# A three-layer graph network on one core: the head's loads put on one queue, and the list of layer 0 set out anew

## The chip, the core and the metric

The kernel runs on one core of a Trainium2 chip. The core has five engines with an instruction stream each: TensorE (PE, with its weight loads PEld), VectorE (DVE), ScalarE (ACT), GpSimd (POOL) and SyncE (SP). SP, ACT and POOL can issue transfers; the transfers run on the core's 16 DMA engines. The metric is the device time of one execution in microseconds (us), as the median over runs of the same kernel. The profile is of one execution of its own.

## The reference

The input is x (2500 nodes of 256 features, float32) and 80,000 edges, src to dst, sorted by dst. Cut to what matters:

```
h = max(layernorm(x), 0); xs = [h]
for W, b in layers 0, 1, 2:                  # W is 512 x 256
    m = concat(h[dst], h[src] - h[dst]) @ W + b
    h = relu(segment_sum(m, dst) / max(count(dst), 1))
    xs.append(h)
out = x + concat(xs) @ Wf + bf
```

No edge list is walked for the messages. With W split into an upper half Wt (for h[dst]) and a lower half Wb (for h[src]), a layer is relu((A z)/count + h (Wt - Wb)), where z = h Wb and A is the 2500 x 2500 matrix of how often each edge occurs. So the kernel builds A once, out of the sorted edges, and uses it in all three layers.

## The kernel before, in words

The work is done by `by_windows` (from L353). `general` (L18) is a fallback that runs only if a count does not add up; nothing of it runs here. Nodes lie in 20 tiles of 128; the code speaks of 10 pairs of tiles, q = 0 to 9. The columns of A (the dst side) are cut into 417 windows of 6 nodes, and these into 5 groups (GWS, four of 84 windows and one of 81); the last group is called "alone" later on.

**The head** has two strands that run side by side up to some 35 us.

The strand of the nodes: x is loaded into `acc` in five chunks of tiles (0-1, 2-5, 6-11, 12-15, 16-19; L443). For each pair: `st` takes mean and variance on DVE (BATCH_NORM_STATS2 and BATCH_NORM_AGGREGATE, tile `st` and `mv`); `sq`, `sc`, `of` turn the variances of a group of pairs into scales on ACT and DVE (groups: pair 0; pair 1; pairs 2-3; 4-7; 8-9); `N`, `Nd`, `Nm`, `Np` normalize the two tiles on POOL, DVE or ACT; `T` transposes them on PE, `R` takes them to `hT` with the relu on ACT; `Z` and `F` are the products with the layer's Wb and with Wf's first part (own_w), each 8 matmuls; `H`, `L` split Z's result into a high part zh (ACT) and a low part zl (DVE), `G` copies F's result into `acc` (ACT).

The strand of the edges: dst is loaded whole as 128 rows of 625 (`dst_i`). `first` and `next` compare row ends, `pi`, `pk`, `sg`, `se` search for the first edge of each block of windows (there are four blocks); `start_i` is the result, `ge` fetches a block's edges with two indirect transfers issued by POOL (`ed`, `es`), `aw`, `ka`, `kb`, `kr`, `km`, `kw`, `kc`, `kt`, `k1`, `k2` turn them into keys. From the keys, `B` makes one-hot tiles on DVE (`one_m`, `one_n`), `C` multiplies them on PE, and `E` copies the counts into A on ACT (`a`). `dstr` and `io` are casts on ACT (dst_i into `dst_r`; index rows).

**What sets the order.** There is no scheduler at work on the compute engines: every operation goes through the wrapper `InOrder` (its line, L267, stands in nearly all rows of the profile), and two strings, `order` and `later` (L920 and L1165), list the steps. Each engine runs the parts of the steps that are its own, in the order of the list, and waits on semaphores for what the other engines do. A short string `PICKS` (L372) says which bank of PSUM each product takes, and `WARM` says ahead of which steps PE runs matmuls on a tile `idle` that only keep it busy. POOL has both the normalizing steps and the indirect transfers in one stream.

**The rest of layer 0** is the string `later`: `g` opens a group of columns, `u` multiplies one tile of nodes into it (4 matmuls of zh and zl against `a`), `o` adds a node's own term, `r` ends the group (relu into `hT`); `c`, `e`, `b` go on with counts, copies and one-hots for the next groups; `f` finishes a group's `a` and writes it to `a_dram` through POOL's queue; `d`, `y`, `p`, `s`, `w`, `l` prepare node degrees, own terms and weights. `k` issues four loads of the next weights from SP into tiles that the one-hots no longer need (`one_m`, `one_n`); `v` makes three forms of the fourth of them, which `q` (products of the last two pairs) needs; `g` of the last group also has SP load the bias `bf_sb`, into memory that group 3's `a` held; `x` has POOL add five tiles of x onto `acc` by a transfer; `h` writes the result of `q` to `acc`.

**Layers 1 and 2** read A back from `a_dram` (tile `staged`), make `block` tiles of it and multiply; the change does not touch their text. Layer 1 begins at about 187 us.

The head's loads, in the order of the program (L432 to L475): ACT's queue issues dst_i and x's tiles 6-11; SP's queue issues x's tiles 0-1 and 2-5, Wb of layer 0, tiles 12-15, Wf's first part, tiles 16-19 (two transfers), Wt of layer 0.

Of the kernel before, what the change touches and what calls it, by code (L numbers as in the profile page):

```python
# [298 lines left out]
def by_windows(ctx: ExitStack, tc: tile.TileContext, x, src, dst, Ws, bs, Wf, bf, out, missing):  # L299
    nc = tc.nc  # L300
    PE, DVE, ACT, POOL, SP = nc.tensor, nc.vector, nc.scalar, nc.gpsimd, nc.sync
    PEo, DVEo, POOLo, ACTo, SPo = (InOrder(tc, e) for e in (PE, DVE, POOL, ACT, SP))
# [57 lines left out]
    class Banks:  # L360
# [9 lines left out]
    left = ctx.enter_context(ExitStack())  # L370
    right = ctx.enter_context(ExitStack())
    PICKS = {  # L372
        "right": "012313013012310102103210321032103210321032103210321032103210321032103210321032103210321032103210321032103210321031",
        "odd": "01010101011010",
        "even": "010101010101101010101010101001100110101010",
    }
    ps_right = Banks(right.enter_context(tc.tile_pool(name="ps_right", bufs=1, space=PSUM, side="right")), 4, PICKS["right"])
    ps_two = [Banks(left.enter_context(tc.tile_pool(name=f"ps_{k}", bufs=1, space=PSUM)), 2, PICKS[k]) for k in ("odd", "even")]
# [52 lines left out]

    dst_rows = dst.rearrange("(p c) -> p c", p=P)  # L432
    dst_i = pp.tile([P, R], I32, name="dst_i")
    ACTo.dma_start(dst_i, dst_rows)
# [9 lines left out]
    load_x(SPo, *chunks[0])  # L444
    load_x(SPo, *chunks[1])
    load_x(ACTo, *chunks[2])
    ws = [None] * L
    wfs = [None] * (L + 1)
    raws = [None] * (L + 1)
# [21 lines left out]
    load_wb(0, SPo)  # L471
    load_x(SPo, *chunks[3])
    load_wf(0, SPo)
    load_x(SPo, *chunks[4])
    load_wt(0, SPo)  # L475

# [57 lines left out]
    first = pp.tile([P, 1], F32, name="first")  # L534
# [358 lines left out]
    def by_count(g):  # L893
# [24 lines left out]
        "B": compare, "C": counts, "E": lambda b: take_counts(b, a),  # L918
    }
    order = """  # L920
        dstr lim first st0 sq0 next pi0 pk00 sc0 pk01 pi1 sg00 of0 Nm0 T0 st1 se00 sg01 pk10 st2 se02 R0 sq1 sc1
        of1 sg10 se01 se03 pk21 sg21 Z0 Np1 pk31 sg31 st4 T1 st7 pk30 sg30 st6 st5 F0 st8 R1 sq3 sc3 pk20 sg20
        se04 pk11 Z1 sg11 Nd7 pb0 T7 se10 ge0 G0 aw0 of3 se11 st3 R7 F1 se12 N6 T6 sa0 se13 ge1 H0 ge3 st9 ka0
        io kr0 kb0 sq4 sc4 km0 kw0 se14 R6 G1 Nm5 F7 kc0 kt0 k10 k20 pb1 of4 Np8 Nm9 L0 G7 H1 T5 R5 sa1 B0 B1 B2
        aw1 F6 G6 B3 kr1 ka1 Z6 kb1 H6 C0 kw1 E0 C1 T9 E1 ka3 sq2 ge2 R9 km1 T8 R8 sc2 B5 B4 L6 Z5 C2 H5 C3 E2
        E3 Z9 L5 C5 N2 C4 kc1 of2 aw2 V9 aw3 L1 E5 km3 H9 E4 B7 B6 T2 Z7 kr2 R2 kt1 k21 ka2 kb2 k11 C6 E6 N4 Z2
        km2 kr3 C7 kb3 kw2 C8 Nm3 T4 E7 kw3 E8 kc2 kc3 T3 B9 kt2 R3 k12 k22 kt3 k23 k13 L9 B8 B11 Z8 B12 C10 H2
        C9 L2 B13 Z3 C11 C12 E10 F3 H7 R4 E9 E12 E11 C13 G3 C14 E14 E13 B10 F5 L7 B15 C16 H8 B17 B19 B16 C15 E15
        G5 L8 E16 Z4 H4 L4 C18 C17 E17 F4 H3 C20 C19 E18 F2 E20 E19
        """  # L930

    second = ctx.enter_context(ExitStack())
# [56 lines left out]
    E12 = 4096.0  # L989
    C1 = 1.0 + 1.0 / E12  # L990
# [160 lines left out]
    def take_next(it=iter(range(len([b for b in windows if b[0] == 0]), len(windows)))):  # L1151
# [11 lines left out]
        "h": each((late_final, (q,)) for q in LATE),  # L1163
    }
    later = """  # L1165
        g d d d B18 u G4 u B23 d d u u G2 u B21 d u B24 ws c e e e e B14 B22 B20 b L3 u d d d b b d u u u c d y
        e e o e o b u b c o o e e u e e w e f b c u u b b d e e e e u c b b d d u u u d w e e e e u c d e d d u
        b b c r g u e u e b w e u u c w b b e y e e e d u u p x u u u c d u u u o e e b b f c e e e b b d o p e
        e e e u u u c d d d u u u o u o b e e b e e c e d b b d u d d r g c e u u u e e y u b b u u u c d d u u
        p u u u b e e e c b y d d b b e o f u c b e e o u e u e e e e u u p d c o d o e e e e b c e e e f d b d  # L1170
        b u u u c b b p r b g u u u u c x u o u u e b b o u u u e c e e e e e e p e o x b b e e e u u u c u u b
        b e c e e o e u b s y b c e e e e u e f k v v v v u u l u r g u s u u u u u u p u q o q o u s p u u o u
        q u u q u u u o u u u n n n n h s h x r l
        """
    acts.update(steps)
    for name in (order + later).split():
# [272 lines left out]
    for l in range(1, L):  # L1449
# [66 lines left out]
    for i, q in enumerate(order):  # L1516
# [30 lines left out]
def gnn_kernel(tc: tile.TileContext, x, src, dst, Ws, bs, Wf, bf, out):  # L1547
    nc = tc.nc
    with tc.tile_pool(name="flag", bufs=1) as flag:
        missing = flag.tile([1, 1], I32, name="missing")  # L1550
        tc.mark_branch_hint_location("again", "LikelyTaken",
                                     engines=[getattr(mybir.EngineType, e) for e in ("PE", "DVE", "Activation")])
        near_end = by_windows(tc, x, src, dst, Ws, bs, Wf, bf, out, missing)
        loads, (again,) = nc.values_load_multi_w_load_instructions(missing, min_val=0, max_val=1)

        for d in loads:
            if d.ins.engine in [getattr(mybir.EngineType, e) for e in ("PE", "DVE", "Activation")]:
                tc.add_manual_dep(d.ins, near_end.ins.name,
                                  mybir.DependencyInfo(mybir.DependencyClass.Sync, mybir.DependencyReason.DATA),
                                  reason="behind the outputs")  # L1560
        with tc.If(again > 0, label="again"):
            general(tc, x, src, dst, Ws, bs, Wf, bf, out)
# [28 lines left out]
```

## Time and profile before

| what | value |
|---|---|
| runs | 458.28, 458.49, 459.91 us; median 458.49 |
| profiled execution | 458.63 us, of which the span from first to last instruction is 456.5 us |
| PE busy | 449.2 us (98% of the span) |
| PEld, DVE, ACT, POOL busy | 358.2, 372.8, 318.9, 43.6 us |
| granted PE clock | 1.000 over the span |
| moved by DMA | 52.47 MB, 115 GB/s over the span; 277 GB/s in the first of 40 slices (11.4 us) |

The page names engine, operation, `out<-in` by the program's tiles, the count of instructions, and idle time with what ended it. Matmuls are pipelined, so their durations overlap, and the start of one against the start of the next tells more than the duration. "SPq", "ACTq" and "POOLq" are the issuing of transfers by these engines. A wait is put down to the one thing that came last by the profile.

### The profile page before, as it was taken

What the parts mean: (1) busy time and instruction counts of PE and PEld (TensorE: products, weight loads), DVE (VectorE), ACT (ScalarE), POOL (GpSimd) and SP (SyncE); (2) the same over time, 40 slices, a digit from 0 to 9 for tenths busy, and PEclk for the clock granted to TensorE, in tenths of its full rate; (3) what the DMA queues carried; (4) which work ended last, traced back from release to release, by engine and by line L of the source; (5) the groups of instructions that cost most, each with busy time, mean ns of one, the idle gap of its engine ahead of it and who ended that gap; (6) DMA issues with size and microseconds to landing.
All of it is one profiled execution on the core that took longest, in us unless ns stands there. A gap on an engine that the chain in (4) does not pass through costs nothing.

```text
span 456.5 us, 7452 instructions
## 1 busy us (share of the span) xinstructions
PE 449.2 (98%) x2737; PEld 358.2 (78%) x2737; DVE 372.8 (82%) x724; ACT 318.9 (70%) x586; POOL 43.6 (10%) x64
## 2 busy tenths in 40 slices
PE   8999999999999999999999999999999999999996
PEld 4888877888888888878878868867888787688685
DVE  6999999998899555379979859876999687569796
ACT  5898878777764535397779849756877897497540
POOL 4790101101022010100000000000000000000000
PEclk9999999999999999999999999999999999999999
DMA  8310266833719985611495522011124855220015
GB/s 277 115 36 1 51 122 111 157 79 70 151 36 192 154 199 103 145 47 45 123 378 204 182 90 93 0 45 47 46 54 142 326 184 180 90 92 1 1 53 176
DMA packets 22056, 52.47 MB, mean 115 GB/s; under 512 B 1931, under 2 KB 12382, under 8 KB 22014
## 3 DMA queue, kind: packets, MB, share of 16 engines
q1 hardware_dynamic: 14654, 33.83, 22.2%
q0 software_dynamic: 5856, 16.48, 19.0%
q10 hardware_dynamic: 1504, 1.63, 1.1%
q8 instruction: 22, 0.36, 0.3%
q14 instruction: 20, 0.16, 0.1%
HBM read 36.47 MB, written 15.62 MB: 114 GB/s over the span
## 4 chain that ended last, share of the span: by engine, by line
PE 89%; DMA 3%; POOL 3%; DVE 3%; ACT 1%; issue 1%; ACTq 0%; POOLq 0%
PE bank L267 89%; DMA acc<-in_x_dram 2%; POOL acc L267 1%; DMA staged<-a_dram 1%; DVE st L267 1%; POOL es L267 1%; POOL ed L267 1%; DVE acc L267 0%; DVE staged L267 0%; DVE mv L267 0%; ACT block L267 0%; DVE tmp L267 0%; ACT tmp L267 0%; DVE zl L267 0%; ACT zh L267 0%
## 5 line engine op out<-in xcount | busy, mean ns | idle before, releaser
L267 ACT CAST block<-staged 128x1008 fp32r<-128x1008 bf16 x120 | 117.9, 1031 | 18.9 <-DVE staged L267 6.5
L267 PE MATMUL bank<-block,zh 128*128 128x504 f32 (+1 forms) x200 | 83.7, 418 | 0.0
L267 PE MATMUL bank<-a,zh 128*128 128x504 f32 (+1 forms) x200 | 80.3, 401 | 0.0
L267 PE MATMUL bank<-a,zl 128*128 128x504 f32 (+1 forms) x200 | 77.9, 389 | 0.0
L267 PE MATMUL bank<-block,zl 128*128 128x504 f32 (+1 forms) x200 | 77.2, 386 | 0.0
L267 ACT CAST a<-bank 128x480 fp32r<-128x480 f32 (+1 forms) x105 | 53.0, 568 | 26.6 <-PE bank L267 26.6
L267 PE MATMUL bank<-block,sh 128*128 128x504 f32 x160 | 69.1, 432 | 0.0
L267 DVE TENSOR_TENSOR one_m<-iota_m,key_m 128x2048 bf16<-128x2048 bf16 (+2 forms) x55 | 63.9, 1162 | 5.9 <-PE bank L267 5.9
L267 PE MATMUL bank<-block,staged 128*128 128x512 f32 (+1 forms) x288 | 62.8, 369 | 0.2 <-DVE staged L267 0.2
L267 PE MATMUL bank<-block,sl 128*128 128x504 f32 x160 | 62.5, 391 | 0.0
L267 PEld LDWEIGHTS bank<-block,staged 128*128 128x128 f32 x288 | 49.3, 189 | 10.6 <-DVE staged L267 0.8
L267 DVE TENSOR_TENSOR block<-staged 128x1008 fp32r<-128x1008 bf16 x40 | 46.9, 1204 | 5.3 <-PE bank L267 3.9
L267 PEld LDWEIGHTS bank<-block,zh 128*128 128x128 f32 x200 | 37.6, 188 | 10.8 <-issue 2.1
L267 PEld LDWEIGHTS bank<-block,zl 128*128 128x128 f32 x200 | 37.6, 188 | 10.5 <-issue 3.5
L267 PEld LDWEIGHTS bank<-a,zl 128*128 128x128 f32 x200 | 37.7, 188 | 7.4 <-issue 0.5
L267 PEld LDWEIGHTS bank<-a,zh 128*128 128x128 f32 x200 | 37.6, 188 | 7.5 <-issue 0.5
L267 DVE TENSOR_TENSOR one_n<-iota_n,key_n 128x640 bf16<-128x640 bf16 (+2 forms) x110 | 42.7, 429 | 0.0
L267 PEld LDWEIGHTS bank<-block,sh 128*128 128x128 f32 x160 | 30.1, 188 | 10.5 <-issue 3.5
L267 PEld LDWEIGHTS bank<-block,sl 128*128 128x128 f32 x160 | 30.1, 188 | 9.3 <-issue 3.7
L267 DVE TENSOR_TENSOR staged<-staged 128x1008 bf16<-128x1008 bf16 x40 | 27.1, 679 | 12.0 <-ACT block L267 11.6
L267 PEld LDWEIGHTS <-one_m 128*128 128x128 bf16 x834 | 29.1, 98 | 7.3 <-issue 4.3
L267 PE MATMUL bank<-own_w,hT 128*128 128x256 f32 x144 | 34.7, 385 | 0.0
(192 smaller groups left out, 645.2 us busy)
## 6 DMA issues: line engine op xcount, KB each, us to landing
staged<-a_dram SPq DMA_DIRECT2D x52, 504.0 KB
a_dram<-a POOLq DMA_DIRECT2D x20, 630.0 KB, 9.0
acc<-in_x_dram POOLq DMA_DIRECT2D x3, 640.0 KB, 17.2
out_dram<-acc SPq DMA_DIRECT2D x5, 256.0 KB
acc<-in_x_dram SPq DMA_DIRECT2D x2, 512.0 KB
acc<-in_x_dram ACTq DMA_DIRECT2D x1, 768.0 KB
out_dram<-acc SPq DMA_DIRECT2D x5, 128.0 KB
wt<-in_L_gnn_W_dram SPq DMA_DIRECT2D x2, 256.0 KB
```

Of the source, the lines that this page charges most:

```text
L267: return self.tc.keep_in_program_order(call(*args, **kwargs))
```

## The change

The two transfers on ACT's queue go to SP's queue, and the order there becomes: tiles 0-1, dst_i, tiles 2-5, Wb, tiles 6-11, Wf's first part, tiles 12-15, tiles 16-19, Wt. The two strings that list layer 0's steps, and the string of PSUM banks, are replaced by others. The same steps are in them; `order` as a whole now ends with the copies of the counts, and pair 2's product F2 has gone over into `later`.

```
     "right": the picks from the 11th on
     "odd":   "01010101011010"           ->  "01010100100101"
     "even":  the picks from the 17th on
 dst_i = pp.tile([P, R], I32, name="dst_i")
-ACTo.dma_start(dst_i, dst_rows)
...
 load_x(SPo, *chunks[0])
+SPo.dma_start(dst_i, dst_rows)
 load_x(SPo, *chunks[1])
-load_x(ACTo, *chunks[2])
...
 load_wb(0, SPo)
-load_x(SPo, *chunks[3])
+load_x(SPo, *chunks[2])
 load_wf(0, SPo)
+load_x(SPo, *chunks[3])
 load_x(SPo, *chunks[4])
 load_wt(0, SPo)
...
 order = """
-dstr lim first st0 sq0 next pi0 pk00 sc0 pk01 pi1 sg00 of0 Nm0 T0 st1 se00 sg01 pk10 st2 se02 R0 sq1 sc1
+lim first dstr io st0 next pi0 pk00 sq0 sc0 of0 pk01 Nm0 sg00 pi1 st1 sg01 T0 R0 st5 sq1 sc1 se00 se02
...
 later = """
-g d d d B18 u G4 u B23 d d u u G2 u B21 d u B24 ws c e e e e B14 B22 B20 b L3 u d d d b b d u u u c d y
+g ws G4 d d L4 d d F2 G2 d d d u u u B24 u B14 B22 u c e B20 u u e e b e d d d u u u b c e u u u b b c d
...
-b e c e e o e u b s y b c e e e e u e f k v v v v u u l u r g u s u u u u u u p u q o q o u s p u u o u
-q u u q u u u o u u u n n n n h s h x r l
+c e e e u u e o u c e s u p u u r g u f o o b k u u u u v u u u u u v v l q n q s p s n n n u u u u u
+q h u u u o q h x o s u u l r x
```

What it makes of three engines' streams:

SP, the loads of the head, as they stood before (own_w_131 is Wb, own_w_134 Wf's first part; dst_i and the 6 tiles were on ACT):

```order
L267 DMA acc<-in_x_dram 128x2x256
L267 DMA acc<-in_x_dram 128x4x256
L267 DMA own_w_131<-in_L_gnn_W_dram 128x2x256
L267 DMA acc<-in_x_dram 128x4x256
L267 DMA own_w_134<-in_L_gnn_Wf_dram 128x2x256
L267 DMA acc<-in_x_dram 128x3x256
L267 DMA acc<-in_x_dram 68x256
L267 DMA wt<-in_L_gnn_W_dram 128x2x256
```

and as they stand in the change:

```order
L267 DMA acc<-in_x_dram 128x2x256
L267 DMA dst_i<-in_dst_dram 128x625
L267 DMA acc<-in_x_dram 128x4x256
L267 DMA own_w_130<-in_L_gnn_W_dram 128x2x256
L267 DMA acc<-in_x_dram 128x6x256
L267 DMA own_w_133<-in_L_gnn_Wf_dram 128x2x256
L267 DMA acc<-in_x_dram 128x4x256
L267 DMA acc<-in_x_dram 128x3x256
```

The chunk of six tiles now stands fifth of one stream, behind dst_i, tiles 2-5 and Wb.

DVE, from the end of pair 1's statistics to the first `start_i` (block 0's) and a little on, before (st and mv are the statistics, end_f the search):

```order
L267 TENSOR_SCALAR end_f_199<-row_204 128x1
L267 BN_STATS st_275<-acc_85 128x6
L267 BN_STATS st_277<-acc_85 128x6
L267 BN_AGGR mv_205<-st_275 128x2
L267 BN_AGGR mv_205<-st_277 128x2
L267 SCALAR_TENSOR_TENSOR end_f_199<-base_197,end_f_199 128x1
L267 RECIPROCAL rs_206<-rs_206 128x2
L267 SCALAR_TENSOR_TENSOR off_207<-mv_205,rs_206 128x2
L267 SCALAR_TENSOR_TENSOR end_f_199<-base_197,end_f_199 128x1
L267 TENSOR_SCALAR start_i_202<-end_f_199,least_203 128x1
L267 BN_STATS st_308<-acc_85 128x6
```

and in the change:

```order
L267 BN_AGGR mv_205<-st_276 128x2
L267 BN_AGGR mv_205<-st_278 128x2
L267 RECIPROCAL rs_206<-rs_206 128x2
L267 TENSOR_SCALAR end_f_199<-row_204 128x1
L267 SCALAR_TENSOR_TENSOR end_f_199<-base_197,end_f_199 128x1
L267 SCALAR_TENSOR_TENSOR off_207<-mv_205,rs_206 128x2
L267 SCALAR_TENSOR_TENSOR end_f_199<-base_197,end_f_199 128x1
L267 BN_STATS st_299<-acc_85 128x6
L267 BN_STATS st_301<-acc_85 128x6
L267 BN_AGGR mv_205<-st_299 128x2
L267 BN_AGGR mv_205<-st_301 128x2
L267 TENSOR_SCALAR start_i_202<-end_f_199,least_203 128x1
```

Before, the pair that follows pair 1 here is pair 2 (tiles 4-5, of the chunk 2-5), and the first row that needs the six tiles is st_308 (pair 4). In the change st_276 and st_278 are pair 5 (tiles 10-11, of the six) and st_299, st_301 pair 4, so that the end of the search and `start_i` now stand behind the statistics of two pairs of that chunk. Pair 2 comes after pairs 6 and 7.

SP, the loads that layer 0's `later` issues, before:

```order
L506 DMA dst_e<-outer 1x128
L267 DMA one_m<-in_L_gnn_W_dram 128x2x256
L267 DMA one_m<-in_L_gnn_Wf_dram 128x2x256
L267 DMA one_n<-in_L_gnn_W_dram 128x2x256
L267 DMA one_n<-in_L_gnn_Wf_dram 128x2x256
L267 DMA bf_sb<-in_L_gnn_bf_dram 128x256
```

and in the change:

```order
L506 DMA dst_e<-outer 1x128
L267 DMA bf_sb<-in_L_gnn_bf_dram 128x256
L267 DMA one_m<-in_L_gnn_W_dram 128x2x256
L267 DMA one_m<-in_L_gnn_Wf_dram 128x2x256
L267 DMA one_n<-in_L_gnn_W_dram 128x2x256
L267 DMA one_n<-in_L_gnn_Wf_dram 128x2x256
```

The load of the bias, which has to wait for the end of group 3, now stands ahead of the four loads of `k` in SP's stream.

More of the change, by code (lines that the diff above doesn't have):

```diff
@@ L433, in by_windows @@
     dst_i = pp.tile([P, R], I32, name="dst_i")
-    ACTo.dma_start(dst_i, dst_rows)
     DVE.memset(acc[:, NT - 1, :], 0.0)
@@ L444, in by_windows @@
     load_x(SPo, *chunks[0])
+    SPo.dma_start(dst_i, dst_rows)
     load_x(SPo, *chunks[1])
-    load_x(ACTo, *chunks[2])
     ws = [None] * L
@@ L471, in by_windows @@
     load_wb(0, SPo)
+    load_x(SPo, *chunks[2])
+    load_wf(0, SPo)
     load_x(SPo, *chunks[3])
-    load_wf(0, SPo)
     load_x(SPo, *chunks[4])
@@ L920, in by_windows @@
     order = """
[L921 to L929, printed above, removed]
+        lim first dstr io st0 next pi0 pk00 sq0 sc0 of0 pk01 Nm0 sg00 pi1 st1 sg01 T0 R0 st5 sq1 sc1 se00 se02
+        pk21 sg21 of1 se01 pk10 sg10 Np1 st4 se03 Z0 pk20 sg20 pk30 T1 R1 F0 sg30 st6 st7 sq3 st2 pk31 sg31 sc3
+        se10 se04 pk11 Nd7 Z1 G0 se11 sg11 of3 st9 pb0 ge0 se12 aw0 T7 F1 R7 st3 sq2 se13 sa0 se14 st8 kr0 pb1
+        H0 Nm5 ka0 N6 kw0 T6 sq4 G1 R6 kb0 kc0 sa1 F7 km0 kt0 k10 ge1 T5 k20 G7 R5 sc4 F6 L0 ge3 of4 Nm9 Z6 Np8
+        T8 B0 T9 B1 B2 aw1 G6 aw3 B3 ka1 kb1 H1 H6 ge2 kr1 C0 E0 ka3 kw1 R9 sc2 B5 B4 C1 kc1 E1 L1 Z5 H5 C3 L5
+        L6 N2 C2 E2 Z9 E3 V9 aw2 C4 km1 R8 of2 C5 T2 E5 R2 B7 km3 Z7 ka2 kt1 kb2 E4 H9 kr3 C6 kr2 k21 kb3 B6 Z2
+        k11 N4 kw2 E6 C7 km2 Nm3 E7 C8 E8 kw3 T4 kc2 T3 R3 kt2 k22 kc3 B9 B8 k12 L9 kt3 Z8 k23 B11 k13 H2 C10 C9
+        B12 E10 E9 Z3 H8 C11 L2 C12 F3 H3 H7 B13 B10 C14 C13 F5 L7 B15 C15 C16 B17 E12 E11 R4 Z4 L8 B19 B16 B18
+        E14 C17 L3 B23 G3 C18 F4 E13 E15 E16 G5 E17 E18 C20 H4 C19 B21 E20 E19
         """
```

22 lines of the change are left out of this document (11 added, 11 removed).

## The prediction

> **What bounds the kernel now.** I read the page's parts 1 and 2 first, then who waits for whom, then the chain of work that ended last.
>
> ```profile
> PE 449.2 (98%) x2737; PEld 358.2 (78%) x2737; DVE 372.8 (82%) x724; ACT 318.9 (70%) x586; POOL 43.6 (10%) x64
> PEclk9999999999999999999999999999999999999999
> PE bank L267 <- DVE idle L519: 1.6, 1, 1.6
> PE bank L267 <- POOL acc L267: 0.7, 1, 0.7
> PE bank L267 <- DVE staged L267: 0.2, 1, 0.2
> ```
>
> PE is busy for 449.2 of 456.5 us at the full granted clock, and it waits three times: 1.6 us at the start, 0.7 us for a tile that POOL normalizes, 0.2 us at the entry of layer 1. A new order of the same matmuls can give back little: these waits, and what PE spends on filling. The filling counts as busy:
>
> ```profile
> L267 PE MATMUL bank<-idle 128*128 128x512 bf16 x15 | 6.0, 546 | 1.6 <-DVE idle L519 1.6
> 30.79 0.41 PE L267 MATMUL bank<-shift,acc 128*128 128x128 f32 x2
> 31.91 0.44 PE L267 MATMUL bank<-shift,acc 128*128 128x128 f32 x2 [0.71 <-POOL acc L267]
> ```
>
> The 15 matmuls on `idle` are in the change too. The transposes of pair 2 show the 0.71 us: the first tile's at 30.79, the second's at 31.91. The chain says what that tile hangs on:
>
> ```profile
> 1.24 9.29 DMA acc<-in_x_dram
> ...
> 10.55 0.75 DVE st L267 x2
> ...
> 17.23 0.19 DVE start_i L267 x2
> 17.41 0.34 DVE st L267
> ...
> 17.86 0.11 POOL ed L267
> ...
> 28.07 3.80 POOL acc L267 x2
> ...
> 31.91 155.17 PE bank L267 x1408
> ```
>
> Read from the top: the six tiles of x land at 10.53; DVE works from there without a gap to the `start_i` of blocks 1 to 3 (end 17.42); POOL fetches edges and normalizes from 17.86 to 31.86; from 31.91 PE runs for 155.17 us without a wait, to the end of layer 0. So the head's length is the time of this one tile, and what comes before it on PE only has to be ready earlier.
>
> **The change, part by part.**
>
> *When the loads land.* Four stretches (the last two columns are the busy share of the DMA engines, in us, and GB/s), and rows that wait for a load (11.40 is T1):
>
> ```profile
> 0.00:4.00 4.00, 2.38 (x6) 0.89 (x7) 1.46 (x13) 1.49 (x2) 3.24 (x20) 1.00 0.51 145
> 0.00:8.60 8.60, 6.71 (x22) 2.68 (x22) 5.39 (x31) 4.05 (x10) 3.98 (x23) 1.00 0.79 252
> 0.00:10.80 10.80, 8.91 (x31) 4.24 (x32) 7.29 (x42) 6.23 (x18) 4.86 (x24) 1.00 0.85 272
> 11.00:13.00 2.00, 2.00 (x12) 1.65 (x12) 2.00 (x10) 1.46 (x7) 1.50 (x3) 1.00 1.06 319
> 4.50 0.15 DVE L267 CAST first<-dst_i 128x1 f32<-128x1 int32 x1 [1.90 <-DMA dst_i<-in_dst_dram]
> 11.40 0.60 PE L267 MATMUL bank<-shift,acc 128*128 128x128 f32 x4
> 12.14 1.59 PEld L267 LDWEIGHTS bank<-own_w,hT 128*128 128x128 f32 x8 [0.22 <-DMA own_w<-in_L_gnn_Wf_dram]
> ```
>
> Moved by 4.0 us: 4.0 x 145 = 580 kB; by 8.6: 2167 kB; by 10.8: 2938 kB. In one stream, dst_i (320 kB behind 262 kB of x) is the 582nd kB, so it is moved by 4.0 us; today it lands a little before 4.50 with the same bytes and some others. I take 4.3: the search starts 0.2 us earlier. The six tiles end at 262 + 320 + 524 + 262 + 786 = 2154 kB: moved by 8.6. How long from moved to landed? Today Wf's part is the last of 2941 kB (all of ACT's 1106, and SP's up to it, 1835), moved by 10.8, and PE sees it at 12.1: 1.3 us. dst_i shows under 0.5 us, early on; the lag grows with the bytes, so between them 1.0: **the six tiles land at 9.6 us**, 0.9 earlier than today. Bounds: 8.6 with no lag, 10.5 as today.
>
> The Trainium skill has a price for a load: "DMA: Bandwidth & Descriptors", "Anatomy of one DMA — SWDGE (gpsimd) path", a fixed 2.0 us plus the bytes at 436 GB/s, fitted on POOL's transfers. An estimate by it from the first issue at 0.73 us is 7.7 us for the same bytes. The trace disagrees (345 GB/s between 4.0 and 8.6 us, and 1.3 us of lag), and I go by the trace; the page's time would make it the first rival below.
>
> *DVE from that landing to `start_i`.* Today:
>
> ```profile
> 9.60 0.13 DVE L267 SCALAR_TENSOR_TENSOR end_f<-base,end_f 128x1 f32<-128x1 f32 x1
> 10.55 0.75 DVE L267 BATCH_NORM_STATS2 st<-acc 128x6 f32<-128x256 f32 x2 [0.23 <-DMA acc<-in_x_dram]
> 14.86 0.17 DVE L267 RECIPROCAL rs<-rs 128x8 f32<-128x8 f32 x1
> 15.14 2.56 POOL L267 TENSOR_SCALAR acc<-acc,mv,rs 128x256 f32<-128x256 f32 x2 [1.30 <-DVE ends L267]
> 17.75 0.31 ACT L267 CAST iota_m<-im_i 128x128 bf16<-128x128 int32 x1
> ```
>
> From 10.55 to 14.86 stand five pairs of statistics, 0.86 us each. Today's stretch to `start_i` holds six pairs and takes 17.42 - 10.55 = 6.87 us. The change has seven pairs after the six tiles (5, 4, 6, 7, 2, 9, 3), and the end of block 0's search, which today fills 9.60 to 10.32 (0.72 us), stands behind the first of them; `lead` (0.1 us) goes behind `start_i`. That is 6.87 + 0.86 + 0.72 - 0.10 = 8.35 us: `start_i` at 9.6 + 8.35 = 17.95, against 17.42. DVE is ready for pair 5 at about 8.5, so it idles 1.1 us where it idled 0.23. POOL today comes to the fetch of block 1 when its two tiles of pair 6 are done, 15.14 + 2.56 = 17.70, and starts it at 17.86. In the change their scales come after five pairs, the search and one small step, 9.6 + 4.30 + 0.72 + 0.4 = 15.0, so POOL is free at 17.6, and the fetch waits for `start_i`: about 18.05. From there to 31.86 POOL's stream is the same sequence of fetches and tiles, without a gap, so pair 2's second tile is **0.2 us later**. Bounds: landing at 8.6, DVE going on at once, gives -0.7; landing at 10.5 gives +1.1 (`start_i` at 18.85). The earlier dst_i is lost in DVE's wait. PE's own way to that point: T1 waits for a tile that POOL starts after pair 5 (9.6 + 0.86 + 0.2, and 1.28 us on POOL), 12.0 instead of 11.40, and F0 at 12.4 instead of 12.14, since Wf's part is no longer late; it arrives 0.3 us later and still has 0.6 us to spare. The casts `io` go from 17.75 on ACT to the start, between `dstr` and pair 0's scale, where ACT has nothing else to do: nothing; if they do delay that scale, it is ahead of DVE's wait for the six tiles and lost in it.
>
> *The steps of `order` and `later` behind that.* The matmuls are the same and F2 only changes place: nothing, as long as PE finds each one's inputs ready. One place has a new reason not to:
>
> ```profile
> 157.46 0.40 SPq L267 DMA_DIRECT2D one_m<-in_L_gnn_W_dram  x1
> 162.70 2.18 POOL L267 DMA_DIRECT2D a_dram<-a  x4 [22.92 <-issue]
> a_dram<-a POOLq DMA_DIRECT2D x20, 630.0 KB, 9.0
> 163.32 0.63 ACT L267 ACTIVATE one_m<-one_n 128x512 fp32r<-128x512 f32 x1 [2.02 <-DMA one_n<-in_L_gnn_Wf_dram]
> 164.17 0.35 SPq L267 DMA_DIRECT2D bf_sb<-in_L_gnn_bf_dram  x1
> 165.35 0.75 ACT L267 ACTIVATE one_m<-one_n 128x256 fp32r<-128x256 f32 x2 [0.16 <-DVE one_n L267]
> 170.68 0.39 PE L267 MATMUL bank<-a,zl 128*128 128x486 f32 x1
> 170.90 0.38 PE L267 MATMUL bank<-a,zh 128*128 128x486 f32 x1
> 171.34 0.39 PE L267 MATMUL bank<-one_m,wt 128*128 128x256 f32 x2
> ```
>
> Today the four loads go out from 157.46 on, the fourth lands at 163.3, its three forms are made by 166.1 (2.8 us), and PE uses them at 171.34, with 5.2 us to spare. In the change SP first has to issue bf_sb, which waits for group 3's end, 164.17. The loads then go out 7.1 us later (164.17 + 0.35 against 157.46), the fourth lands at 170.4, the forms are ready at 173.2. PE comes to them later too: after the first `q` the new list (its last two rows stand in the diff) has 10 `u` and 2 `o` where the old has 12 and 4, at 0.22 us a matmul (170.68 to 170.90) 8 x 0.22 + 6 x 0.22 = 3.1 us less to go, so at 171.34 + 3.1 + 0.2 = 174.6. That leaves 1.4 us: I take **0**. But the writes of `a_dram`, which today start when the loads have landed, now start among them; bound: the landing slips past the point where the wait begins, 171.8, by 1 us, +1.
>
> *The entry of layer 1.*
>
> ```profile
> 182.35 2.26 POOL L267 DMA_DIRECT2D acc<-in_x_dram  x2 [17.47 <-ACT acc L267]
> 187.10 1.08 ACT L267 ACTIVATE hT<-bank 128x486 f32<-128x486 f32 x2 [4.70 <-PE bank L267]
> 188.08 0.61 ACT L267 COPY wt<-one_n 128x512 f32<-128x512 f32 x1
> 188.72 4.91 DMA staged<-a_dram
> ```
>
> The first load of `staged` goes out behind ACT's copy of `wt`. The new list has `l` ahead of `r`, so the copy runs under the last two `u` and the load goes out at 188.2, 0.5 us earlier; PE's wait behind it is 0.2 us (and a gap of about 0.3 with it): at best -0.5. Against it, the additions of x's last tiles now hang on `h` at the very end of layer 0 (about 185.5 instead of 182.35), and would still be moving when `staged` loads: up to +1 us. I take **0**.
>
> *The sum* against the profiled execution: 458.63 + 0.2 + 0 + 0 = 458.8; that execution is 0.14 us above the median of the runs, so **458.7 us**.
>
> **The rivals.**
>
> *The six tiles land when they are moved* (8.6), or before DVE is ready. For it: the wait of dst_i leaves hardly a lag. Against: Wf's 1.3 us. Then -0.7 in the head and -0.5 at layer 1: 457.3. The skill's figure above would have it so.
>
> *One queue does not carry what two did*, and the six tiles come no earlier than today. For it: 319 GB/s when SP alone has loads left, against 345 between 4.0 and 8.6 ((2167 - 580) / 4.6). Then +1.1 in the head: 459.6. The same skill page, "Issuing engines are not separate DMA queues", says all queues share the same 16 engines, so one should do; no run here shows one queue from the start.
>
> *Slower: the loads held behind bf_sb.* If the writes of `a_dram` take the engines first, the fourth load lands with them: issued at 166 to 168, with a median of 9.0 us to landing, they are done at 177; forms at 179.8, PE waits 5.2 us: 463.8. It decides from a landing at 171.8 on, 1 us for 1 us; past 174.1 it is over 0.5%. Against: `f`, which starts the writes, stands one `u` behind the opening of the last group, so that the loads go out about 1 us before them.
>
> *The change gives more than I see.* All of PE's waits after the start (0.9 us) gone, and half of the filling (3.0 of 6.0 us) not needed as the search starts sooner: 454.7. Against: `WARM` is as before, and dst_i cannot come much before 4.0.
>
> **How the numbers follow.** Forecast 0.50 (own range 457.9 to 459.6), early landing 0.25, late landing 0.14, loads held 0.08, more than I see 0.03. The range that leaves out the last two but takes in the first three with 0.4 us of spread around them (the runs lie from 458.28 to 459.91): 456.9 to 460.6. About 0.5% (2.3 us) is what a measurement of this kernel can tell from no change. Beyond it on the fast side lies only the last case, with a little for what I did not walk: faster 0.05. On the slow side the held loads and a little more: slower 0.09. Same: 0.86.
>
> **What would show it.** In the changed kernel's profile DVE's first statistics behind pair 1 wait about 1 us for `acc<-in_x_dram` and start near 9.6; the fetch of block 1 on POOL starts near 18.0; PE waits 0.6 to 0.9 us for `acc` from POOL at pair 2's second transpose, near 32.1; bf_sb goes out ahead of the four loads near 164 and PE has no wait at `one_m,wt`; the first `staged` load goes out near 188.4. I am wrong if statistics start before 9 or after 10.2, if PE waits for `one_m` near 175, or if layer 1's entry shows a wait of more than 1 us.

## The result and the profile after

The changed kernel takes **479.05 us** (median of six runs, 477.54 to 481.27), the kernel before beside it 458.51: 1.0441 times as long, with a 95% interval of 1.0401 to 1.0480 (here and in the table below the ratio is not the quotient of the two medians). The forecast was 458.7, with a range up to 460.6. In a second series (below) it takes 477.69 us, ratio 1.0412 (1.0395 to 1.0428).

The profiled execution took 480.26 us, of which the span is 478.4: 21.9 us more than before. From its page, parts 1 and 2, and from the view of PE's waits:

```profile
PE 454.1 (95%) x2737; PEld 361.9 (76%) x2737; DVE 372.8 (78%) x724; ACT 318.5 (67%) x586; POOL 44.5 (9%) x64
PEclk9899999999999995799999999999999999999999
PE bank L267 <- ACT one_m L267: 13.6, 3, 12.9
PE bank L267 <- POOL acc L267: 3.2, 3, 2.4
PE bank L267 <- DVE idle L519: 1.6, 1, 1.6
PE bank L267 <- DVE staged L267: 1.3, 2, 1.1
```

Where PE waited 0.7, 1.6 and 0.2 us, it now waits 3.2, 1.6 and 1.3, and 13.6 us in a place that had no wait at all: for `one_m` from ACT, the forms of the fourth early load. The clock is no longer full in two places, and PE is busy 4.9 us longer with the same 2737 matmuls. The chain of waits of the changed kernel, cut to its long pieces:

```profile
2.77 8.57 DMA acc<-in_x_dram
...
11.36 0.75 DVE st L267 x2
...
20.55 0.11 DVE start_i L267 x2
...
35.65 131.70 PE bank L267 x1290
...
168.34 1.77 SPq L267
...
173.42 16.68 DMA one_n<-in_L_gnn_Wf_dram
...
192.68 15.04 PE bank L267 x68
...
208.23 7.23 DMA staged<-a_dram
...
221.84 252.08 PE bank L267 x1094
```

Beside the chain of before, the 21.9 us divide by stage. PE's run behind pair 2's second tile begins at 35.65 and not at 31.91: the head, +3.7. From there to the end of layer 0 (207.72, before 187.08) it is 172.1 against 155.2: +16.9. From there to PE's first long run in layer 1 (221.84, before 200.00) 14.1 against 12.9: +1.2. The rest is the same (252.08 and 252.10). Of the head's 3.7 us some 2.5 belong to this execution: in the profile of the second series the last matmul of group 3 ends at 164.88, here at 167.35.

The large piece is a load of 256 KB that is 16.68 us under way. This is what happens around it, first on SP's queue and POOL's, then what PE and ACT wait for:

```profile
167.88 0.37 SPq L267 DMA_DIRECT2D bf_sb<-in_L_gnn_bf_dram  x1
168.34 1.77 SPq L267 DMA_DIRECT2D one_m<-in_L_gnn_W_dram  x1
173.42 1.39 SPq L267 DMA_DIRECT2D one_n<-in_L_gnn_Wf_dram  x1
167.46 1.58 POOL L267 DMA_DIRECT2D a_dram<-a  x3 [24.64 <-issue]
169.89 1.56 POOL L267 DMA_DIRECT2D acc<-in_x_dram  x1
190.18 0.63 ACT L267 ACTIVATE one_m<-one_n 128x512 fp32r<-128x512 f32 x1 [21.11 <-DMA one_n<-in_L_gnn_Wf_dram]
190.87 0.58 PE L267 MATMUL bank<-one_m,wt 128*128 128x256 f32 x1 [12.91 <-ACT one_m L267]
```

The first of the four loads goes out at 168.34 (before 157.46), 0.9 us behind the first writes of `a_dram`, and the third addition of x follows at once. The view of stretches, for the time from then to the landing (last two columns: busy share of the DMA engines, GB/s):

```profile
168.00:190.00 22.00, 9.96 (x46) 8.14 (x44) 0.00 (x0) 1.05 (x2) 3.12 (x4) 0.79 1.00 201
```

22 us at 201 GB/s are 4.42 MB. The four loads are 1.05 MB, bf_sb 0.13, the four writes 2.58 (630 KB each), the addition of x 0.66: together 4.42 MB. So the DMA engines are busy the whole time (a share of 1.00) with just these, and the fourth load ends with the last of them.

### The profile page after: what moved, and what is told of

It reads as the page before. It is cut to its first block, busy times and chain, and to the rows that moved or that the text cites. A ratio compares the mean times of both kernels' runs of the same rounds, so it can differ in the third digit from the quotient of the medians.

```text
span 478.4 us, 7454 instructions
## 1 busy us (share of the span) xinstructions
PE 454.1 (95%) x2737; PEld 361.9 (76%) x2737; DVE 372.8 (78%) x724; ACT 318.5 (67%) x586; POOL 44.5 (9%) x64
## 4 chain that ended last, share of the span: by engine, by line
PE 84%; DMA 7%; POOL 3%; DVE 2%; SPq 1%; ACT 1%; issue 1%; ACTq 0%; POOLq 0%
PE bank L267 84%; DMA one_n<-in_L_gnn_Wf_dram 3%; DMA acc<-in_x_dram 2%; POOL acc L267 2%; DMA staged<-a_dram 2%; SPq L267 1%; POOL es L267 1%; POOL ed L267 1%; ACT one_m L267 0%; DVE st L267 0%; DVE staged L267 0%; DVE acc L267 0%; ACT hT L267 0%; ACT block L267 0%; DVE tmp L267 0%
## 5 line engine op out<-in xcount | busy, mean ns | idle before, releaser
L267 PEld LDWEIGHTS bank<-block,zl 128*128 128x128 f32 x200 | 37.6, 188 | 10.5 <-issue 3.4
L267 PEld LDWEIGHTS bank<-block,sh 128*128 128x128 f32 x160 | 30.1, 188 | 10.5 <-issue 3.5
```

What stands on the lines that cost most here:

```text
L267: return self.tc.keep_in_program_order(call(*args, **kwargs))
```

## The experiments

| kernel | us, median | ratio to before beside it, 95% interval |
|---|---|---|
| the change, second series | 477.69 | 1.0412 (1.0395 to 1.0428) |
| bias's load behind the early loads | 461.28 | 1.0040 (1.0024 to 1.0056) |
| writes held until the loads have landed | 461.39 | 1.0041 (1.0023 to 1.0059) |
| before, with bias's load ahead | 475.69 | 1.0341 (1.0307 to 1.0374) |
| before, with the change's loads in the head | 459.59 | 1.0009 (0.9993 to 1.0024) |
| bias behind, head's loads on two queues | 461.21 | 1.0031 (1.0016 to 1.0045) |
| bias behind, end of the list earlier | 459.28 | 0.9993 (0.9982 to 1.0005) |
| bias behind, pair 5's statistics later | 465.36 | 1.0082 (1.0050 to 1.0113) |
| both of the last two | 464.13 | 1.0114 (1.0099 to 1.0129) |
| both, and a step between the comparisons | 459.60 | 1.0025 (1.0013 to 1.0037) |
| the change, wait filled with 52 matmuls | 476.66 | 1.0369 (1.0348 to 1.0391) |
| the change, wait filled with 66 | 476.50 | 1.0390 (1.0375 to 1.0405) |
| the change, T1's wait filled | 477.16 | 1.0403 (1.0388 to 1.0417) |
| bias behind, six tiles behind Wf | 461.65 | 1.0067 (1.0052 to 1.0083) |
| the same, T1's wait filled | 461.07 | 1.0048 (1.0032 to 1.0063) |

The ratio of "pair 5's statistics later" leaves out the two longest of its twelve runs (466.56 and 466.95 us); the median is of all twelve.

### Layer 0: the four loads

**The order on SP's queue undone.** bf_sb's load goes to the end of `early_loads`, nothing else:

```
 def begin():
-    SPo.dma_start(bf_sb[0], ...)
 def early_loads():
     SPo.dma_start(late_w[0], ...)
+    SPo.dma_start(bf_sb[0], ...)
```

> The changed kernel with one transfer moved: bf_sb's load is issued behind the four early loads, so that these no longer stand behind a load that waits for the end of group 3. Theory A (SP's order: the four loads went out 10 us later and so among the writes of a_dram): they go out from about 160.7, when the one-hots' last full product but one has freed their tiles, the fourth lands by 168, its forms are ready by 171, PE comes to them at about 178 and waits for nothing. That takes away the 12.9 us of wait, 0.7 us of gaps behind it and the 3.4 us that the half clock cost: 479.1 - 17.0 = 462.0 us. Rival B (the new list itself: it puts the writes and the third addition of x among the loads wherever they stand): the fourth lands after 178 all the same, and the time is 468 us or more.

461.28 us. In its timeline (SP's queue, then ACT):

```profile
157.93 0.40 SPq L267 DMA_DIRECT2D one_m<-in_L_gnn_W_dram  x1
165.59 0.35 SPq L267 DMA_DIRECT2D bf_sb<-in_L_gnn_bf_dram  x1
166.81 0.63 ACT L267 ACTIVATE one_m<-one_n 128x512 fp32r<-128x512 f32 x1
```

The loads go out even earlier than theory A had it, land before the writes have begun to matter, and PE has no wait at `one_m`. By the ratios, one transfer's place on the queue is worth 3.7 to 4.0% of the 4.1 to 4.4% lost (the two series of the change), some 17 to 18 us. Rival B falls.

**The order left, the company taken away.** bf_sb stays ahead, but POOL holds group 4's writes (and, behind them, the addition of x) back:

```
 def finish(g):
     ACTo.copy(a[PAD:PAD + 1, NT - 1, :n], ...)
+    if late_w:
+        POOLo.tensor_copy(landed, late_w[0][0:1, 0, 0:1])
 later:
-g u f o o b k u u u u v
+g u o o b k f u u u u v
```

> The changed kernel with bf_sb's load ahead of the four early loads as in the change, but group 4's writes of a_dram held on POOL until the fourth load has landed (POOL first copies one element of it). Theory A1 (the loads are late because they share the DMA engines with 3.2 MB of writes and additions): alone, they go out from 168.3 and land by 174, the forms are ready by 177, PE waits at most 0.5 us where it waited 12.9: 462 to 463 us. Rival A2 (they are late because they go out late and slowly, the writes matter little): the fourth lands after 180, and at least 8 of the 17 us stay: 470 us or more.

461.39 us, the same gain by the other way. Here the loads go out 8 us later than in the run before, and land 6 us after the first issue:

```profile
165.96 1.11 SPq L267 DMA_DIRECT2D one_m<-in_L_gnn_W_dram  x1
172.03 0.18 POOL L267 COPY landed<-one_n 1x1 f32<-1x1 f32 x1 [31.56 <-DMA one_n<-in_L_gnn_Wf_dram]
174.63 1.56 POOL L267 DMA_DIRECT2D acc<-in_x_dram  x1
```

So going out late alone costs nothing here: that much of the forecast's step (0, with 1.4 us to spare) holds, if only just, since the last of the forms is ready at 174.9 and PE comes to them at 175.4. Going out late *into the writes* costs 17 us. Either edit mends it.

**The same fault put into the kernel before.** The step `k` and what hangs on it go behind the opening of the last group:

```
-u e f k v v v v u u l u r g u s
+u e f u u u r g k v v v v l u s
```

> The kernel before with the four early loads, their forms and the step l put behind the opening of the last group, so that bf_sb's load stands ahead of them as in the change; head, banks and the rest of the list are as before. Theory A (order on SP, and the engines shared with the writes): the loads go out from about 164.5, behind the start of the writes at 162.7, the fourth lands at 180 to 183, the forms come 2.5 us later, PE waits 11 to 14 us at 171.3 and runs at a lower clock behind that: 472 to 477 us. Rival B (the new list's shape is needed for it): the fourth lands by 171 and the time is 458.5 to 461 us.

475.69 us. Neither the head's loads nor the new list is needed for the loss, nor the addition of x, which is not among the transfers here:

```profile
163.07 2.18 POOL L267 DMA_DIRECT2D a_dram<-a  x4 [22.92 <-issue]
164.54 0.37 SPq L267 DMA_DIRECT2D bf_sb<-in_L_gnn_bf_dram  x1
181.82 0.63 ACT L267 ACTIVATE one_m<-one_n 128x512 fp32r<-128x512 f32 x1 [16.70 <-DMA one_n<-in_L_gnn_Wf_dram]
```

PE waits 13.3 us (by the profile for ACT's `wt`, which stands behind the forms in ACT's stream). The sum of bytes holds here too: four loads, bf_sb and four writes are 3.76 MB, and from 163 to 182 the DMA engines moved 199 GB/s, 3.78 MB.

### The clock behind the wait

Of the 16.9 us in layer 0, 12.9 are the wait and 0.7 two gaps behind it. That leaves 3.3 us, and the clock accounts for most of them: matmuls that follow each other in 0.22 us before the wait take 0.41 us behind it, up to 197.8. To see what the idle time itself did, extra matmuls were put ahead of the first late product:

```
     late_banks[q] = bank()
+    if q == LATE[0]:
+        for i in range(52):      # 66 in the second kernel
+            PEo.matmul(late_banks[q][:, :n], tile_of(zh, i % 20)[:, :P], as_[g][:, i % 20, :n], start=True, stop=True)
```

> The changed kernel, with 52 extra matmuls ahead of the first product on the late weights (a times zh into the bank that this product then overwrites; nothing of the result is left out), so that PE is busy for 52 x 0.22 = 11.4 of the 12.9 us in which it waits for the forms. Theory G (the idle time itself made the clock fall: granted 0.50 from the wait on until 197.8): the clock stays at 1.00, the wait is as long, and the 3.4 us that the half clock cost behind it, with some of the gaps between the first products, come back: layer 0 ends about 3.6 us earlier, 475.4 us, ratio 1.036. Rival H (the clock falls for the load on the DMA engines or something else that goes on in that stretch): it falls all the same, and the time stays at 479 us or grows.

The ratio of 1.0369 is what theory G gave, and still this run does not show what G says. The head of the profiled execution was shorter by some 3 us, so that the loads went out and landed 3 us earlier, and behind the filled wait the clock fell all the same. The stretches of 1 us:

```profile
186.00:187.00 1.00, 0.54 (x3) 0.12 (x1) 0.00 (x0) 0.00 (x0) 0.00 (x0) 1.00 0.13 38
187.00:188.00 1.00, 0.22 (x1) 0.19 (x1) 0.24 (x1) 0.63 (x1) 0.00 (x0) 1.00 0.00 0
188.00:189.00 1.00, 0.48 (x2) 0.19 (x1) 0.85 (x3) 0.76 (x2) 0.00 (x0) 0.91 0.00 0
189.00:190.00 1.00, 0.58 (x3) 0.41 (x3) 1.00 (x3) 0.88 (x3) 0.00 (x0) 0.50 0.00 0
```

(PE's busy time first, the clock third from the end.) The 52 matmuls end at 186.5; what is left of the wait and the two gaps behind it are 2.2 us in three pieces, and by the 0.91 of the third row the clock fell at about 188.8, when 1.8 us of them were past. From the last of the forms (189.59) to the end of layer 0 (205.13) it took 15.5 us, no less than the 15.0 of the change. So the fill was made longer, to reach over the gaps too:

> The changed kernel with 66 extra matmuls ahead of the first late product, where the run before had 52 and left PE idle for 2.2 us between the end of these and the third of the forms; 66 x 0.22 = 14.5 us reach to the last of the forms (nothing of the result is left out). Theory G1 (any stretch of some 2 to 3 us that is mostly idle lowers the clock, and it comes back only after about 7 us of work): the clock stays at 1.00 between 176 and 200 us, and layer 0 ends 13.0 us after the last of the forms, where that took 15.1 us in the change and 15.5 us with 52: 474.4 us. Rival H1 (the clock falls for another reason in this stretch): it falls again, 15 us or more from the last of the forms to the end of layer 0, 476.7 us.

From the chain of waits, and from the stretches of 4 us:

```profile
190.67 12.85 PE bank L267 x68
```

```profile
188.00:192.00 4.00, 3.88 (x23) 3.20 (x21) 2.19 (x6) 3.13 (x7) 0.00 (x0) 1.00 0.00 0
```

Now the same 68 steps of the chain take 12.85 us, against 15.04 in the change, at a clock of 1.00 throughout. Idle time on PE lowers the clock, whatever the DMA engines do meanwhile, and its price in this stage is 2.2 us. The time as a whole does not show it: 476.50 us is no better than the 476.66 of the shorter fill (by the ratios it is 0.2% worse), whose gain lies elsewhere, in the entry of layer 1: 13.1 us against 14.2 in the second series, for which no run here shows a reason. The longer fill also missed G1's 474.4, which was reckoned from the first series. Beside the second (477.69) it gains 1.2 us; in the profiles 0.7 of the 2.2 us go to a later landing (25.5 us from group 3's end to the last of the forms, against 24.8 in the change's second series). The Trainium skill, "TensorE: Matmul & The Clock Gate", "Part 1: The HAM clock gate", has the clock at half behind an idle window of about 3.4 us and full again after about as long of work. The half and the cause agree; here 1.8 us of idle time within 2.3 us were enough, and by stretches of 1 us the full clock was back 5.0 us behind the last of the forms in the change and 6.1 us with the 52 matmuls. A single wait of 1.60 us (T1 with the bias's load behind) left it at 1.00.

### The head

**The loads alone,** in before's list:

```
-ACTo.dma_start(dst_i, dst_rows)          (and tiles 6-11, on ACT)
+SPo: x 0-1, dst_i, x 2-5, Wb, x 6-11, Wf, x 12-15, x 16-19, Wt
```

> The kernel before with the head's loads on SP's queue in the order of the change, and nothing else changed. Theory C (one queue carries less than two do in the first 9 us, 269 to 322 GB/s against 305 to 375): the six tiles land at about 11.3 as in the change, DVE idles about 1 us ahead of the fourth pair's statistics, and the head is 0.8 us longer: 459.3 us. Rival D (the landing is late only together with the new list): they land by 10.5, 458.5 us.

The median cannot be told from no change. The profiled execution (460.51 us) shows a delay, but not the one of theory C:

```profile
10.73 0.75 DVE L267 BATCH_NORM_STATS2 st<-acc 128x6 f32<-128x256 f32 x2 [0.42 <-DMA acc<-in_x_dram]
13.03 0.76 DVE L267 BATCH_NORM_STATS2 st<-acc 128x6 f32<-128x256 f32 x2 [1.32 <-DMA acc<-in_x_dram]
```

The six tiles land 0.2 us later than before, and the chunk behind them (tiles 12-15, now behind Wf) makes DVE wait once more.

**The two queues of before under the new list** (with the bias's load behind):

> The changed kernel with bf_sb's load behind the four early loads, and the head's loads on the two queues of before, in before's order. Theory J (the head's loss is the landing of what one queue carries): 459.8 to 460.5 us, with the six tiles at 10.5 and the later chunks 1.7 us earlier. Rival I (it is the order of the list: pair 5's statistics wait for the six tiles wherever they are issued, and these land at 10.5 on both): T1 waits 1.5 us as before, 461.0 to 461.5 us.

461.21 against 461.28 us: the number of queues is not what the head's loss hangs on. The six tiles are at 10.54, and T1 still waits 0.93 us for POOL, less than the 1.5 of rival I. Theory J falls, I stands.

**Pair 5's statistics behind pair 1's normalization** (bias's load behind):

```
-T0 R0 st5 sq1 sc1 se00 se02 pk21 sg21 of1 se01 pk10 sg10 Np1 st4 se03
+T0 R0 sq1 sc1 se00 se02 pk21 sg21 of1 se01 pk10 sg10 Np1 st5 st4 se03
```

> The changed kernel with bf_sb's load behind the four early loads (461.3 us, ratio 1.004), and pair 5's statistics (which wait for the six tiles) put behind pair 1's scale and normalization in the list. Theory I (T1's wait of 1.6 us is one of order: pair 1's scale stands on DVE behind statistics that wait for the six tiles): T1 runs at about 11.4 without a wait; POOL's chain comes only about 0.9 us earlier, since the small steps of the search leave DVE's stretch behind the landing, so that some 0.4 us come back as a wait at pair 2: 460.1 us, ratio 1.0015. Rival J (the head's loss is the landing, not the order): T1 no longer waits, but the same time is lost at pair 2's tile, and it stays at 461.3 us.

465.36 us: worse, against both theories. T1 no longer waits, and `start_i` is 0.7 us earlier, as I said. But the runs lie in two lots, four at 459.6 to 461.9 and eight at 465.1 to 467.0, and in the profile of one of the eight PE waits 3.9 us for POOL at pair 8:

```profile
22.96 5.04 POOL L267 DMA_INDIRECT es<-src_e,start_i  x1 [0.31 <-issue]
22.75 0.51 DVE L267 TENSOR_TENSOR one_n<-iota_n,key_n 128x320 bf16<-128x320 bf16 x2
23.18 1.22 DVE L267 TENSOR_TENSOR one_m<-iota_m,key_m 128x2048 bf16<-128x2048 bf16 x1
26.17 0.80 DVE L267 TENSOR_TENSOR one_n<-iota_n,key_n 128x640 bf16<-128x640 bf16 x2
```

A fetch of edges that takes 1.0 to 1.4 us in the other kernels takes 5.04. It ends at 28.00, 1.03 us after DVE's row of comparisons does (26.97), and 1.03 us is what it takes in the kernel that this one was made from. So it looks as if it had not begun before.

**The end of the list earlier** (bias's load behind):

```
-q h u u u o q h x o s u u l r x
+q h q h x x u u u o o s u u l r
```

> The changed kernel with bf_sb's load behind the four early loads, and the last late product, its final step and the last addition of x put 8 u and 2 o ahead, so that this addition (0.6 MB by POOL's queue) is issued near 183 and not at 187.35. Theory K (the first staged load of layer 1, 7.56 us against 4.91, shares the engines with this addition): it takes about 4.9 us again, the entry's wait of 1.4 us goes, 459.9 us, ratio 1.001. Rival L (it is late for other reasons, the order on SP among them): it stays above 7 us, 461.3 us.

459.28 us, no longer to be told from before. With the last addition of x out at 184.10 and not at 187.35, the wait for `staged` is gone from PE's list:

```profile
184.10 2.24 POOL L267 DMA_DIRECT2D acc<-in_x_dram  x2 [14.92 <-ACT acc L267]
```

```profile
PE bank L267 <- POOL acc L267: 2.3, 2, 1.6
PE bank L267 <- DVE idle L519: 1.6, 1, 1.6
```

**All three edits, and a step between the comparisons** (a normalization on DVE, `Nm9`, moved behind block 0's):

```
-ge3 of4 Nm9 Z6 Np8 T8 B0 T9 B1 B2
+ge3 of4 Z6 Np8 T8 B0 Nm9 T9 B1 B2
```

> The three edits together: bf_sb's load behind the four early loads, pair 5's statistics behind pair 1's normalization, and the last late product and the last addition of x ahead in the list. With the statistics alone, POOL's fetch of the third block's sources took 5.04 us in the profile where the others took 1.0 to 1.5, and the runs lay at 459.6 to 461.9 or at 465.1 to 467.0 us. Theory M (that fetch is shut out while DVE runs its one-hot comparisons without a break, and comes through only where it starts before them): the runs lie in the same two lots, 2 us earlier each: 457.6 to 459.9 and 463 to 465 us. Rival N (it was an accident of the other edit): one lot at 458 us.

> As the run with the three edits, with one more: a normalization on DVE (a TENSOR_SCALAR of 0.41 us with one tensor as input) stands between the one-hot comparisons of block 0 and those of the next ones, where it stood ahead of them. Theory M1 (the comparisons in an unbroken row shut out POOL's fetch, and a step of another kind lets it through): the fetch takes 1.5 us or less, all runs lie at 457.5 to 458.5 us, ratio 0.997. Rival N1 (a gap of one step does not let it through): the fetch takes 4 to 5 us in most runs and these lie at 462.5 to 465 us.

Without the step all runs lie at 463.7 to 464.2 us and the fetch takes 5.04 us again: M's upper lot, no lower one. With it the fetch takes 1.07 and the runs lie at 458.8 to 461.1, one lot, though not at M1's 458:

```profile
23.25 0.41 DVE L267 TENSOR_SCALAR acc<-acc,mv,rs 128x256 f32<-128x256 f32 x1
23.08 1.07 POOL L267 DMA_INDIRECT es<-src_e,start_i  x1 [0.30 <-issue]
26.91 1.09 PE L267 MATMUL bank<-shift,acc 128*128 128x128 f32 x8 [1.40 <-POOL acc L267]
```

The last row says where the rest went: T1 waits no more, but PE then waits 1.40 us for POOL's tile of pair 8 and begins its long run at 26.91, where it begins at 26.90 with T1's wait in it. POOL's chain behind `start_i` is the bound there; PE's early wait only hid it. That is what theory J had said of pair 2's tile. None of these kernels beats before by more than can be told.

**T1's wait and the two lots of the change.** The first six runs lie at 477.5 to 477.8 and at 480.3 to 481.3 us, three each.

```
-WARM = {"next": 7, "pk00": 3, "T0": 3, "Z0": 2}
+WARM = {"next": 7, "pk00": 3, "T0": 3, "Z0": 2, "T1": 3}      (8 in the last kernel)
```

In the last two kernels of the table the bias's load is behind, and Wf's part goes ahead of the six tiles:

```
 load_wb(0, SPo)
+load_wf(0, SPo)
 load_x(SPo, *chunks[2])
-load_wf(0, SPo)
```

> The changed kernel with three idle matmuls (1.2 us) ahead of T1, whose wait of 2.42 us was followed by the clock at 0.50 from 13.8 to 17 us in the profile of the change; nothing else. Theory G2 (the runs of the change lie in two lots, 477.5 to 477.9 and 480.3 to 481.3 us, because the six tiles land earlier or later and T1's wait is then under or over what lowers the clock): with the wait cut to 1.2 us or less the clock stays at 1.00 in the head and all runs lie at 477 to 478.3 us. Rival J2 (the two lots come from the landing itself and from POOL's chain behind it): half of the runs still lie above 480 us.

> The changed kernel itself once more, as a control beside the next two. Its first runs lay in two lots (477.5 to 477.8 and 480.3 to 481.3 us), and its profile, of the upper lot, shows the six tiles at 11.36 us where seven kernels with the same order of loads and the same start of the list show them at 9.98 to 10.73. Theory G2 (the landing decides: T1 then waits over 2 us and the clock falls): two lots again, or one at 477 to 478 us; a profile of the lower lot shows the landing before 10.8, T1's wait under 1.8 us and the clock at 1.00 in the head. Rival P (the lots come from another place): a profile of the lower lot shows a landing after 11 and the clock fallen in the head, or one of the upper lot neither.

> The changed kernel with bf_sb's load behind the four early loads (461.3 us), and the six tiles of x put behind Wf's first part on SP's queue, 262 kB later, so that they land at about 11.4 and T1 waits 2.4 us in nearly every run. Theory G2 (a wait of this length lowers the clock to 0.50 for about 3 us): the head is longer by the landing (0.75 us) and by 1.5 us of half clock: 463.5 us. Rival P (the clock in the head is of no account): 462.0 us.

> The run before with eight idle matmuls (0.21 us each, 1.7 us) ahead of T1, so that PE waits 0.7 us and not 2.4. Theory G2: the landing's part stays and the clock's is gone: 462.0 us, clock 1.00 in the head. Rival P: as the run before within 0.3 us.

The profile of the upper lot has the landing at 11.36 and T1 behind a wait of 2.42 us, with the clock down behind it:

```profile
13.79 1.12 PE L267 MATMUL bank<-shift,acc 128*128 128x128 f32 x4 [2.42 <-POOL acc L267]
```

```profile
14.00:16.00 2.00, 2.00 (x8) 1.73 (x8) 2.00 (x10) 1.05 (x5) 1.35 (x2) 0.50 0.11 34
```

The second series of the change has one lot (477.0 to 478.5). Its profile has the landing at 10.43, no wait at T1 and the clock at 1.00:

```profile
10.43 0.75 DVE L267 BATCH_NORM_STATS2 st<-acc 128x6 f32<-128x256 f32 x2 [1.50 <-DMA acc<-in_x_dram]
```

```profile
14.00:16.00 2.00, 2.00 (x11) 1.81 (x10) 2.00 (x12) 1.52 (x7) 1.66 (x3) 1.00 0.31 86
```

That agrees with G2, but the kernels made to force it did not get there. With the six tiles behind Wf they landed at 11.05, PE waited only 0.48 us at T1 and the clock stayed (461.65 us against the 463.5 of G2); with the fill they landed at 10.53, and the time (461.07) differs from the run before by less than 0.2%. With T1 filled in the change the landing was at 10.70, early in any case, and the three matmuls took 0.6 us and not 1.2. So the upper lot goes with a late landing and a lower clock in the one profile that shows it; that the clock makes its 3 us is argued, not shown.

## Why the prediction was wrong, step by step

**The step that failed: the loads behind bf_sb, taken at 0.** The edit was seen, its place and its direction too. The landing was put at 170.4 by moving today's 5.9 us along with the issue; the bound for the company of the writes was 1 us. It came to 190.1. The rival "held behind bf_sb" named the mechanism and put the landing at 177, by the median of 9.0 us from issue to landing of one write. But four such writes go out together, 2.58 MB, and the list had also brought the third addition of x to this place, which the working missed. All of the 4.42 MB at the 198 and 219 GB/s that the profile of before has between 166 and 174, while the writes run, takes 21 us from 168 on: 189, about 1 us from what came.

```profile
166.00:170.00 4.00, 4.00 (x19) 3.41 (x19) 2.22 (x8) 1.56 (x4) 0.00 (x0) 1.00 1.00 198
170.00:174.00 4.00, 4.00 (x25) 3.63 (x24) 0.00 (x0) 0.15 (x1) 0.00 (x0) 1.00 1.05 219
```

The bytes stood in the row that was quoted (630.0 KB, x20). "The loads go out about 1 us before them" was wrong by 2 us as well: the writes went out at 167.46, 0.9 us before the loads. The one `u` that stands ahead of `f` in the list did not hold POOL back (PE's first matmul of it is at 167.64), and bf_sb went out only at 167.88. The chance of 0.08 was too low for a step whose outcome hung on which of two queues came first by 1 us.

**The half clock behind a long wait** was in no term, so that even the held-loads rival would have come out 2 us or more too low with the right landing.

**The six tiles at 9.6 us** (bounds 8.6 to 10.5): 11.36 in the first profile of the change, 10.43 in the second, 9.98 to 10.73 in nine other kernels that load in this order. The bytes were right; the rate and the lag from moved to landed were not. Before, 345 GB/s stood for this stretch, and 1.0 us was taken for the lag. By the second row the 2154 kB were moved soon after 9.2 us, not by 8.6, and landed 2 us later; in the second series they were moved by 9.0 and landed 1.5 us later:

```profile
4.00:8.60 4.60, 4.50 (x18) 2.01 (x16) 3.93 (x16) 3.46 (x12) 0.75 (x4) 1.00 0.94 286
0.00:9.20 9.20, 7.48 (x26) 3.28 (x27) 5.74 (x31) 5.49 (x16) 3.98 (x23) 1.00 0.74 231
```

**dst_i 0.2 us earlier**: 4.47 against 4.50 for the first cast on it; the search gained nothing, as the forecast lost it anyway.

**DVE's 8.35 us from the landing to `start_i`** was right: from 10.60 to the end of `start_i` at 19.04 (the end is what the forecast counted) it is 8.44 us in the kernel with the bias's load behind. In the first profile of the change it took 9.3 us, with 0.75 of waiting on ACT.

**PE at T1**, foretold at 12.0 and counted as nothing, came at 13.79 behind a wait of 2.42 us in the first profile of the change, at 12.86 with no wait in the second, and at 13.03 behind 1.60 us with the bias's load behind. The order was read rightly (pair 1's scale stands behind statistics that wait), but PE was given slack "as long as it only has to be ready earlier". A kernel whose PE is 98% busy has none, except where, as here, the next bound (POOL's tile at 26.9) lies within 1.4 us.

**The entry of layer 1 at 0** (-0.5 to +1): it came to +1.2, by the collision that the working named, the addition of x's last tiles with the first `staged` load (7.23 us against 4.91). Moving the addition 3 us ahead took it away. Here the mechanism was right and the size outside its bound by 0.2.

All that was foretold as a sign of error is in the profile: statistics that start after 10.2 (11.36), PE waiting for `one_m` (foretold near 175; it waits from 177.96 to 190.87), and more than 1 us at layer 1's entry (1.1 in the longer of two waits).

## What to carry to other kernels

When a load moves behind another that waits, ask which transfers will be under way when it is let go, add up the bytes of all of them, and divide by the rate that these queues show; the time from issue to landing of one transfer says nothing about the last of several. A long wait of TensorE costs more than its own length: behind 12.9 us of waiting stood another 5 us at half clock, 2.2 us lost in that stage, while a wait of 1.60 us left the clock as it was. Filling such a wait kept the clock only when the fill reached to its very end and over the small gaps behind it, and the whole kernel gained 1.2 us by it. And a stall that is taken away at one engine is worth only the distance to the next bound: here 1.6 us at T1 were worth nothing.

## What the runs showed of the hardware

An indirect fetch that POOL issued 0.8 us into an unbroken row of two-input comparisons on DVE took 5.04 us in two kernels, to 1.03 us past the end of that row; the same fetch issued 0.1 to 0.7 us into the row took 1.0 to 1.4 us in the eleven other profiles of the new list, and issued 0.9 us into it with one TENSOR_SCALAR of 0.41 us between the comparisons 1.07. The Trainium skill, "SBUF — State Buffer", "Who interferes with whom", lets an operation of two inputs in SBUF hold off POOL's reads but (inferred there) not its making of descriptors. Here the fetch seems to have been held off, as the step between the comparisons brought it back; by which of the two, and why at 0.8 us and not at 0.7, cannot be told from these rows.

SP's issue of a 256 KB load took 0.40 to 0.47 us with the DMA engines free (before, and with the bias's load behind) and 0.8 to 1.9 us while the writes were under way (six profiles), so that in the change the four issues took 6.5 us instead of 1.9.
